# A selective scan feeding two attention layers: later groups' projection moved into the scan's steps, weight sums spread by a matmul, the last chunk's output steps moved closer

## The chip, the cores and the metric

The kernel runs on one core of one Trainium2 chip, in one launch. The metric is device time in microseconds, the median of several executions. One further execution was recorded by the hardware profiler; its time stands beside the median in the table below.

## The reference, cut to what matters

The input x has 32 sequences of 256 positions and 256 channels. A state-space block (a scan over positions) runs first, then two layers of windowed attention with a feed-forward part, and x is added at the end.

```
xr, gate = split(x @ W_in.T);  xr += t_emb
xc = silu(causal_conv4(xr) + b_conv)
xn = (xc - mean) / sqrt(var + eps) * ln_g + ln_b
Bm, Cm, dt = split(xn @ W_xproj.T);  dt = tanh(dt @ W_dt.T + b_dt) * 0.01
Ad = 1 + dt * -tanh(A_log);  Bd = Bm * min(|xn|, 1)
h_t = clip(h_{t-1} * Ad_t + Bd_t * xn_t, -10, 10);  y_t = C_t . h_t      # 256 steps
y = (y + D * xn) * silu(gate) @ W_out.T
for l in 0, 1:  y = ffn_l(attention_l(y))
return x + y
```

## The kernel before, in words

**Groups and chunks.** The 32 sequences are worked in 4 groups of 8 (GB). A group's scan has 256 steps, cut into 8 chunks of 32 (CH), and each chunk into two halves of 16 (hb). The partitions of the state h are 16 states by 8 sequences; its 512 columns are the inner channels. Group 0's scan has no attention beside it (`alone`); its tail and the scans of groups 1 to 3 run beside the attention of the group before.

**Slots.** `group_scan` writes an agenda: `at(s, what, ...)` puts a piece of work into slot s, where slot t is the slot of step t. Slots below 0 are preparation. Each group has two agendas; in each slot the pieces of the first come before those of the second. `scan_slots` merges the agendas of all groups, the next group 256 slots later, and `scan_to(s)` emits all slots up to s. This is the program order. The framework's planner then orders each engine's instructions by its own model of when operands and buffers are ready, in which it prefers program order; instructions wrapped in `keep_in_program_order` aren't overtaken. Loads that wait for nothing are drawn forward: weight loads (L978) written for slot 100 and later are issued from 18 us on. [...]

**Preparation of a chunk** (slots s0-43 to s0-4, s0 being the chunk's first step): `load_x` (L455, SP), `project` (L399, PE) into PSUM, `conv_in` (L469 to L483: DVE adds the conditioning, POOL the first tap), `conv_taps` (L489, DVE), `conv_th` (L499, ACT's Silu), `raw_sums` (L518, PE), then for each half j of the chunk's rows `norm_turn` (tp_x, L548, PE), `norm_stats` (L558 to L565, DVE and a power on POOL), `norm_shift` (L571), `norm_apply` (L579, ACT), `norm_affine` (L586 and L587, POOL), `norm_out` (L591 writes the rows to DRAM, xnd, through SP; L593 their squares on ACT). `length`, `figures`, `figures_out` (ps_st, L618), `figures_in` (L630 to L636), `decay_th` and `decays` (L643 to L661) make the steps' coefficients beta, ct and lim.

**Steps.** A step needs the normalised row of each sequence on the partitions of all 16 states. For 24 of 32 steps, `load_rows` (L685, xrep<-xnd, SP) fetches it by DMA six slots ahead; for the others `load_skip` (xq<-xnd, L745, SP) brings 16 rows at once and `spread_rows` (bx, L693, PE) spreads them. `scale_row` (L706, ACT) multiplies by beta, `step` (L716, one custom DVE instruction) makes h, and `read_out` (y, L728, PE) multiplies four steps' h by C.

**Output of a half or chunk:** `gated` (L779, DVE), `out_turn` (tz, L785, PE), `out_gate` (zT, L799, DVE), and after both halves `project_y` (ps_out, L808, PE), `copy_y` (L819, ACT) and `put_y` (L830, ys<-yo, ACT's queue). `load_res` (L956, res<-ys, SP) reads a sequence back for attention, whose first operation is `project_qkv` (ps_qkv, L989, PE).

**Weight sums.** Once, in preparation, `constants` folds W_dt into W_xproj (`fold_1`, `fold_2`: L266 to L284) and needs the column sums of the folded weights on the partitions of the states. `widen_w` (L290, POOL) copies 16 columns to 128 by repeating each 8 times; `sum_w` (tw, L301, PE) multiplies that by two columns (ones, and ln_b). This is done for three parts and two weight tables: six wide copies and 48 matmul instructions (an f32 matmul is two in the profile). `sums_w` (L310 to L312, DVE) reads the sums.

**Projection ahead.** While group 0's scan runs alone, the first half of `project` for the other three groups is done too: 48 units (u), each `ahead_project` (ps_a, L426: 8 matmul instructions), `ahead_copy` (L437, ACT) and `ahead_put` (ahead<-xs_a, L442, SP); every second unit first loads x (xa, L415, two DMAs on SP).

**From scan to attention.** `scan_to(S + DRAIN)` emits slots to 274, the eight `load_res` follow, then six rounds of `project` for attention with one slot each, and then attention stage by stage. Group 1's remaining slots are spread evenly over 114 stages.

Of the kernel before, what the change touches and what calls it, by code (L numbers as in the profile page):

```python
# [20 lines left out]
S = 256  # L21
# [3 lines left out]
NC_ = DI // P  # L25
NS = 16
GB = 8
# [3 lines left out]
NQ = 4  # L31
# [21 lines left out]
def bc(ap, axis, n):  # L53

    ap = ap.unsqueeze(axis)
    shape = list(ap.shape)
    shape[axis] = n
    return ap.broadcast_to(shape)
# [15 lines left out]
def kernel(  # L74
# [147 lines left out]
    def program(ctx, exact):  # L222
# [14 lines left out]
        def constants(at):  # L237
# [25 lines left out]
            def fold_1():  # L263
                td = bank(ps_w, "w", "td")
                for c in range(NC_):
                    nc.tensor.transpose(  # L266
                        td[0:NS, c * P : (c + 1) * P], tmp["wx"][:, c, 2 * NS :], ident
                    )
                wdT = work("swp", "wdT", 3)
                nc.vector.tensor_copy(wdT[0:NS], td[0:NS])  # L270
                tmp["wdT"] = wdT

            def fold_2():
                td = bank(ps_w, "w", "td2")[:, 0 : NC_ * NS].rearrange(
                    "p (c n) -> p c n", c=NC_
                )
                for c in range(NC_):
                    nc.tensor.matmul(
                        td[:, c], tmp["wdT"][0:NS, c * P : (c + 1) * P], tmp["dt"],
                        start=True, stop=True,  # L280
                    )
                wx = tmp["wx"]
                nc.vector.tensor_copy(wx[:, :, 2 * NS :], td)
                nc.vector.tensor_mul(wx_sb[:, :, 0 : 3 * NS], wx, bc(tmp["g"], 2, 3 * NS))  # L284

            def widen_w(i, k):
                t = ap_.tile([P, NC_, NS, GB], FP, tag="swp", name="wide", bufs=3)
                src = (wx_sb, tmp["wx"])[k]
                tc.keep_in_program_order(
                    nc.gpsimd.tensor_copy(t, bc(src[:, :, i * NS : (i + 1) * NS], 3, GB))  # L290
                )
                tmp["wide"] = t

            def sum_w(i, k):
                if (i, k) == (0, 0):
                    tmp["tw"] = bank(ps_w, "w", "tw")[:, 0:12].rearrange(
                        "p (i k n) -> p i k n", i=3, k=2
                    )
                t = tmp.pop("wide")
                for c in range(NC_):  # L300
                    nc.tensor.matmul(  # L301
                        tmp["tw"][:, i, k],
                        t[:, c].rearrange("p n b -> p (n b)"),
                        tmp["cols"][:, c, :],
                        start=(c == 0),
                        stop=(c == NC_ - 1),
                    )

            def sums_w():
                nc.vector.tensor_copy(wsum, tmp["tw"][:, :, 0, 0])  # L310
# [44 lines left out]
            at(-43, load_w)  # L355
            at(-34, fold_1)
            at(-32, fold_2)
            for n in range(6):
                at(-28 + 2 * n, widen_w, n // 2, n % 2)
                at(-27 + 2 * n, sum_w, n // 2, n % 2)  # L360
            at(-14, sums_w)
            at(-19, decay_rate)
            at(-16, load_later)
# [13 lines left out]
        def group_scan(g):  # L377
# [205 lines left out]

            def norm_affine(c, j):
                xn = ck[c]["xn", j]
                nc.gpsimd.tensor_mul(xn, xn, lng_sb)  # L586
                nc.gpsimd.tensor_add(xn, xn, lnb_sb)  # L587

            def norm_out(c, j):
                xn = ck[c].pop(("xn", j))  # L590
# [111 lines left out]
            def scale_row(c, t):  # L702
                if by_tensor(t):
                    ck[c]["rep", t] = xp.tile([P, DI], FP, tag="xrep", name="xrep")
                bx = ck[c]["rep", t]
                scaled = nc.scalar.activation(  # L706
                    bx, ck[c].pop(("bx", t), bx), AF.Copy, scale=ck[c]["beta"][:, t : t + 1]
                )
                if not alone:

                    tc.keep_in_program_order(scaled)

# [140 lines left out]
            for c in range(NCH):  # L853
                for t in range(CH):
                    at(c * CH + t, step, c, t)
            for c in range(NCH):
                s0 = c * CH
                for hb in range(CH // TB):
                    s = s0 + hb * TB
                    for i in range(NI):  # L860
                        at(s + 4 * i + 5, read_out, c, hb, i)
                    at(s + 21, gated, c, hb)
                    at(s + 25, out_gate, c, hb)
                    at(s + 11, skip, c, hb)
                for ch in range(NC_):
                    at(s0 - 38 + 2 * ch, conv_in, c, ch)
                    at(s0 - 37 + 2 * ch, conv_taps, c, ch)
                    at(s0 - 36 + 2 * ch, conv_th, c, ch)
                    if not alone:
                        at(s0 - 35 + 2 * ch, conv_out, c, ch)  # L870
                for ch, s in enumerate((13, 16, 17, 18)):
                    at(s0 + s + 2, gate_th, c, ch)
                    if not alone:
                        at(s0 + s + 4, gate_out, c, ch)
                at(s0 - 25, raw_copy, c)
                at(s0 - 24, raw_turn, c)
                for j in range(NJ):
                    s = s0 - 26 + 4 * j
                    at(s + 2, norm_stats, c, j)
                    at(s + 4, norm_shift, c, j)  # L880
                    at(s + 5, norm_apply, c, j)
                    at(s + 6, norm_affine, c, j)
                    at(s + 9, norm_out, c, j)
                at(s0 - 11, length, c)
                at(s0 - 9, figures, c)
                at(s0 - 7, figures_in, c)
                at(s0 - 6, decay_th, c)
                at(s0 - 5, decays, c)
                at(s0 - 4, put_c, c, 0)
                at(s0 + 4, put_c, c, 1)  # L890
                for d in range(KM):
                    at(s0 + 45 + 2 * d, copy_y, c, d)
                    at(s0 + 46 + 2 * d, put_y, c, d)
            agendas.append({})
            for c in range(NCH):
                s0 = c * CH
# [19 lines left out]
                for hb in range(CH // TB):  # L916
                    s = s0 + hb * TB
                    at(s - 9 if alone else s + 7, load_skip, c, hb)
                    at(s + 23, out_turn, c)
                for d in range(KM):  # L920
                    at(s0 + 43 + 2 * d, project_y, c, d)

            if alone:
                n = (NG - 1) * NCH * 2
                for u in range(n):
                    s = -30 + u * (NCH * CH) // n
                    at(s - 5, ahead_load, u)
                    at(s, ahead_project, u)
                    at(s + 2, ahead_copy, u)
                    at(s + 4, ahead_put, u)  # L930
# [561 lines left out]
                done[0] = next(scan, 1 << 30)  # L1492


        DRAIN = 18
        for i, (kind, k) in enumerate(WEIGHTS):
            scan_to(100 + 8 * i)
            load_weights(0, kind, k)
        scan_to(S + DRAIN)
        for b in range(GB):  # L1500
            load_res(0, b)
        for w in range(NW):
# [135 lines left out]
```

## Time and profile before

| what | us |
|---|---|
| median of 3 runs (3616.05 to 3620.17) | 3618.64 |
| the profiled execution | 3624.1 |
| its span, first to last instruction | 3622.3 |
| step 0 (first L716) starts | 56.93 |
| step 32, 64, 96, 128 | 106.77, 155.84, 204.90, 254.81 |
| step 160, 192, 224 | 303.99, 352.11, 400.44 |
| step 256, group 1's first | 447.77 |
| first ps_qkv | 480.27 |

PE is TensorE's matmuls, PEld its weight loads, DVE VectorE, ACT ScalarE, POOL GpSimd, SP SyncE; SPq and ACTq are DMA issues on those queues. L716 is line 716 of the kernel. Lines of the chain of waits give start, length and what; lines of the timeline give start, length, engine, line, operation, names, shapes, count and, in brackets, idle time before.

### The profile page before, as it was taken

To read this page: it belongs to the slowest core of one execution; us is meant where nothing else is said; L and a number is where in the kernel's file an instruction comes from. 1 tells how busy PE (TensorE), PEld (TensorE's weight loads), DVE (VectorE), ACT (ScalarE), POOL (GpSimd) and SP (SyncE) were. 2 spreads that over 40 slices of the span, in tenths; PEclk is the share of its full clock that TensorE was granted. 3 is DMA by queue.
4 is the path that set the end of the run, shared out by engine and by line. 5 is a ranking of instruction groups with operands and counts; after the bars stand their busy time and mean duration, and the time that the engine had idled before them with its cause. 6 is when DMAs were issued, how large, how long until landed. Compare 5 with 4: busy or idle time off the path is not lost.

```text
span 3622.3 us, 56212 instructions
## 1 busy us (share of the span) xinstructions
PE 3510.2 (97%) x19548; PEld 2282.4 (63%) x19548; DVE 2666.1 (74%) x5049; ACT 2151.6 (59%) x3659; POOL 1801.9 (50%) x1746
## 2 busy tenths in 40 slices
PE   8999989999999999999999999999999999999999
PEld 5445335666666666666666666666666677777677
DVE  5888889888787877887787778877777545555553
ACT  3666656666666666666666666666666444544443
POOL 4333456545455555645455556455544454544551
PEclk8999989999999999999999999999999999999999
DMA  7888755445454645444454554544454112011111
GB/s 192 212 218 217 197 155 149 133 111 137 129 141 123 154 137 151 123 113 128 118 139 125 137 150 135 137 107 130 115 138 120 54 45 62 13 30 36 34 27 37
DMA packets 468763, 435.59 MB, mean 120 GB/s; under 512 B 228724, under 2 KB 308085, under 8 KB 468341
## 3 DMA queue, kind: packets, MB, share of 16 engines
q1 hardware_dynamic: 384018, 419.88, 42.9%
q10 hardware_dynamic: 84450, 12.01, 2.0%
q8 instruction: 158, 2.59, 0.3%
q14 instruction: 137, 1.11, 0.1%
HBM read 383.54 MB, written 46.66 MB: 119 GB/s over the span
## 4 chain that ended last, share of the span: by engine, by line
PE 63%; DVE 16%; DMA 7%; POOL 6%; ACT 4%; issue 3%; SPq 1%; ACTq 0%; DVEq 0%; POOLq 0%
PE ps_qkv L989 13%; PE pa L1351 13%; PE po_f L1378 7%; DVE h L716 6%; DMA xrep<-xnd 5%; PE ps_wo L1039 4%; PE y L728 4%; PE sc L1198 4%; PE ov L1247 3%; PE ps_out L808 3%; PE tr_qk L1028 2%; DVE acc L489 2%; ACT xrep L706 2%; PE rs L1228 2%; PE ps_in L399 2%
## 5 line engine op out<-in xcount | busy, mean ns | idle before, releaser
L716 DVE CUSTOM_DVE_ANT_0 h<-h,xrep,lim 128x512 f32<-128x512 f32 x1024 | 954.0, 932 | 233.7 <-ACT xrep L706 198.4
L706 ACT ACTIVATE xrep<-xrep,beta 128x512 f32<-128x512 f32 x960 | 674.0, 717 | 367.4 <-DMA xrep<-xnd 280.8
L989 PE MATMUL ps_qkv<-qkv,res 128*128 128x512 f32 x1536 | 718.6, 603 | 22.2 <-DVE ag L1369 9.9
L1351 PE MATMUL pa<-hT,w 128*128 128x256 f32 (+1 forms) x2816 | 680.1, 383 | 1.2 <-ACT oT L1254 0.4
L1351 PEld LDWEIGHTS pa<-hT,w 128*128 128x128 f32 (+1 forms) x2816 | 515.3, 188 | 147.1 <-issue 57.1
L1013 POOL TENSOR_TENSOR rot<-rot,swp 128x512 f32<-128x512 f32 x256 | 335.7, 1311 | 444.7 <-DVE swp L1010 339.0
L989 PEld LDWEIGHTS ps_qkv<-qkv,res 128*128 128x128 f32 x1536 | 281.7, 191 | 314.2 <-issue 241.8
L1021 POOL TENSOR_TENSOR rn<-ss,neg_half 128x8 f32<-128x8 f32 x256 | 459.5, 1795 | 17.9 <-DVE ss L1019 7.9
L728 PE MATMUL y<-h,ly 128*32 128x512 f32 x2048 | 346.5, 611 | 12.5 <-DVE h L716 11.4
L1303 POOL TENSOR_TENSOR rstd<-ve,neg_half 128x2 f32<-128x2 f32 x64 | 46.3, 723 | 608.2 <-DVE ve L1301 605.0
L1378 PE MATMUL po_f<-ag,w 128*128 128x256 f32 x1280 | 307.9, 388 | 4.9 <-DVE fo L1389 4.9
L1022 POOL TENSOR_TENSOR rot<-rot,rn 128x512 f32<-128x512 f32 x256 | 291.8, 1140 | 20.1
L1369 DVE SCALAR_TENSOR_TENSOR ag<-pa,b_sb,ag 128x256 f32<-128x256 f32 x320 | 152.6, 477 | 198.8 <-ACT ag L1362 198.6
L1378 PEld LDWEIGHTS po_f<-ag,w 128*128 128x128 f32 x1280 | 236.5, 191 | 69.2 <-issue 12.8
L1002 ACT ACTIVATE sq<-ps_qkv 128x512 f32<-128x512 f32 x256 | 151.7, 596 | 210.1 <-PE ps_qkv L989 148.9
L1362 ACT ACTIVATE ag<-pa,b_sb 128x256 f32<-128x256 f32 x320 | 150.1, 469 | 176.3 <-PE pa L1351 173.9
L489 DVE SCALAR_TENSOR_TENSOR acc<-xr,wc_sb,acc 128x256 f32<-128x256 f32 x384 | 193.4, 528 | 57.6 <-POOL acc L478 57.1
L1039 PE MATMUL ps_wo<-oT,wo 128*128 128x256 f32 x1024 | 231.7, 379 | 0.7 <-ACT ag L1362 0.7
L1005 DVE TENSOR_TENSOR rot<-ps_qkv,rc_sb 128x512 f32<-128x512 f32 x256 | 175.1, 684 | 77.0 <-ACT sq L1002 76.7
L1198 PE MATMUL sc<-qT,kT 64*128 64x128 f32 (+1 forms) x2048 | 220.5, 344 | 0.0
L1207 ACT ACTIVATE pT<-sc 128x512 f32<-128x512 f32 x384 | 208.5, 596 | 12.2 <-PE sc L1198 10.2
L1198 PEld LDWEIGHTS sc<-qT,kT 64*128 64x128 f32 x2048 | 150.8, 187 | 99.8 <-issue 92.7
(159 smaller groups left out, 5656.2 us busy)
## 6 DMA issues: line engine op xcount, KB each, us to landing
xrep<-xnd SPq DMA_DIRECT2D x960, 256.0 KB
rb<-inv SPq DMA_DIRECT2D x128, 256.0 KB
xnd<-xn SPq DMA_DIRECT2D x64, 256.0 KB
qkv<-in_wqkv_dram SPq DMA_DIRECT2D x24, 512.0 KB
ahead<-xs_a SPq DMA_DIRECT2D x48, 256.0 KB
xp<-ahead SPq DMA_DIRECT2D x48, 256.0 KB
xd<-xnd SPq DMA_DIRECT2D x192, 64.0 KB
w<-in_w_dram SPq DMA_DIRECT2D x80, 128.0 KB
```

What stands on the lines that cost most here:

```text
L489: nc.vector.scalar_tensor_tensor(acc, xr[:, :, k : k + CH], wc_sb[:, ch, k : k + 1], acc, ALU.mult, ALU.add,)
L706: scaled = nc.scalar.activation(bx, ck[c].pop(("bx", t), bx), AF.Copy, scale=ck[c]["beta"][:, t : t + 1])
L716: nc.vector._custom_dve(TENSOR_ADD_SAT, out=h_new, in0=state["h"], in1=bx, s0=ck[c]["lim"][:, 0, t : t + 1], s1=ck[c]["lim"][:, 1, t : t + 1],
L728: nc.tensor.matmul(ck[c]["y", hb][32 * q : 32 * q + 32, :], ly[hb % 2][:, 32 * t : 32 * t + 32], ck[c].pop(("h", hb * TB + t)), start=(i = ...
L989: nc.tensor.matmul(ps, res[b][:, k, t0 : t0 + W], wt["qkv", a][:, k], start=(k == 0), stop=(k == KM - 1),)
L1013: nc.gpsimd.tensor_add(rot, rot, swp)
L1021: nc.gpsimd.tensor_tensor(rn, ss, neg_half, ALU.pow)
L1022: nc.gpsimd.tensor_mul(rot, rot, bc(rn, 2, DH))
L1039: nc.tensor.matmul(po[:, d], wt["wo", 0][:, c, d * P : (d + 1) * P], oT[:, c, :], start=(c == 0), stop=(c == NC_ - 1),)
L1198: nc.tensor.matmul(banks[r][:, i, :], kT[rows, i0 + i, kw * W : (kw + 1) * W], qT[rows, i0 + i, kw * W :], start=self.apart, stop=self.apa ...
L1351: nc.tensor.matmul(dst[x], wt["w1", m][:, k, x], self.h[:, k], start=(k == 0), stop=(k == KM - 1),)
L1378: nc.tensor.matmul(self.po[:, d], wt["w2", 0][:, m, d * P : (d + 1) * P], self.ag[m], start=(m == 0), stop=(m == len(MCH) - 1),)
```

## The change

Five things, all in group 0's scan and its two ends.

1. *Weight sums.* `sum_w` now multiplies the 16 columns themselves by the two columns (48 matmul instructions with 16 columns of weights, into 16 partitions); `copy_w` copies the result to SBUF (DVE) and builds a 16x128 matrix of repeated unit columns (POOL); `spread_w` spreads the sums to 128 partitions with one matmul. Two PSUM copies in `fold_1` and `fold_2` go from DVE to ACT.
2. *Projection ahead.* Unit u stands in slot 2 + 246u/48 and no longer in slot -30 + 256u/48.
3. *Chunk 0 and 1.* The affine part for the second half of chunk 0's rows is on DVE; the first eight `scale_row` of chunk 0 are kept in program order; chunk 1's conv steps are two slots later.
4. *The last chunk's second half.* gated, turn and gate stand 19, 20 and 21 slots after its first step (21, 23 and 25 before); the projections 38 and 39 after the chunk's first step (43 and 45), copies 39 and 40 (45 and 47), puts 40 and 41 (46 and 48).
5. *To attention.* `load_res` follows slot 266, not 274. `DRAIN` for later groups is the same.

```diff
-                nc.vector.tensor_copy(wdT[0:NS], td[0:NS])
+                nc.scalar.copy(wdT[0:NS], td[0:NS])
...
-                nc.vector.tensor_copy(wx[:, :, 2 * NS :], td)
+                nc.scalar.copy(wx[:, :, 2 * NS :], td)
...
-            def widen_w(i, k):
...
-            def sum_w(i, k):
...
+            def sum_w():
+                tw = bank(ps_w, "w", "tw")[0:NS, 0:12]
+                for i in range(3):
+                    for k, src in enumerate((wx_sb, tmp["wx"])):
+                        for c in range(NC_):
+                            nc.tensor.matmul(
+                                tw[:, 4 * i + 2 * k : 4 * i + 2 * k + 2],
+                                src[:, c, i * NS : (i + 1) * NS],
+                                tmp["cols"][:, c, :],
+                                start=(c == 0),
+                                stop=(c == NC_ - 1),
+                            )
+                tmp["tw"] = tw
+
+            def copy_w():
+
+                t = ap_.tile([P, NC_, NS, GB], FP, tag="swp", name="wide", bufs=3)
+                tmp["of_state"] = t[0:NS, 0].rearrange("p n b -> p (n b)")
+                tmp["by_state"] = t[0:NS, 1].rearrange("p n b -> p (n b)")[:, 0:12]
+                nc.gpsimd.tensor_copy(t[0:NS, 0], bc(ident[0:NS, 0:NS], 2, GB))
+                nc.vector.tensor_copy(tmp["by_state"], tmp.pop("tw"))
+
+            def spread_w():
+                tw = bank(ps_w, "w", "tw")[:, 0:12]
+                nc.tensor.matmul(tw, tmp["of_state"], tmp["by_state"], start=True, stop=True)
+                tmp["tw"] = tw.rearrange("p (i k n) -> p i k n", i=3, k=2)
...
-            for n in range(6):
-                at(-28 + 2 * n, widen_w, n // 2, n % 2)
-                at(-27 + 2 * n, sum_w, n // 2, n % 2)
+            at(-20, sum_w)
+            at(-19, copy_w)
+            at(-18, spread_w)
...
-                nc.gpsimd.tensor_mul(xn, xn, lng_sb)
-                nc.gpsimd.tensor_add(xn, xn, lnb_sb)
+                e = nc.vector if alone and (c, j) == (0, 1) else nc.gpsimd
+                e.tensor_mul(xn, xn, lng_sb)
+                e.tensor_add(xn, xn, lnb_sb)
...
-                if not alone:
+                if not alone or (c == 0 and t < 2 * NQ):
 
                     tc.keep_in_program_order(scaled)
...
+            def soon(c, hb):
+
+                return alone and (c, hb) == (NCH - 1, CH // TB - 1)
+
...
-                    at(s + 21, gated, c, hb)
-                    at(s + 25, out_gate, c, hb)
+                    at(s + (19 if soon(c, hb) else 21), gated, c, hb)
+                    at(s + (21 if soon(c, hb) else 25), out_gate, c, hb)
...
-                    at(s0 - 38 + 2 * ch, conv_in, c, ch)
-                    at(s0 - 37 + 2 * ch, conv_taps, c, ch)
-                    at(s0 - 36 + 2 * ch, conv_th, c, ch)
+                    s = s0 - 36 if alone and c == 1 else s0 - 38
+                    at(s + 2 * ch, conv_in, c, ch)
+                    at(s + 1 + 2 * ch, conv_taps, c, ch)
+                    at(s + 2 + 2 * ch, conv_th, c, ch)
...
-                    at(s0 + 45 + 2 * d, copy_y, c, d)
-                    at(s0 + 46 + 2 * d, put_y, c, d)
+                    s, q = (s0 + 39, 1) if soon(c, 1) else (s0 + 45, 2)
+                    at(s + q * d, copy_y, c, d)
+                    at(s + 1 + q * d, put_y, c, d)
...
-                    at(s + 23, out_turn, c)
+                    at(s + (20 if soon(c, hb) else 23), out_turn, c)
                 for d in range(KM):
-                    at(s0 + 43 + 2 * d, project_y, c, d)
+                    s, q = (s0 + 38, 1) if soon(c, 1) else (s0 + 43, 2)
+                    at(s + q * d, project_y, c, d)
...
-                    s = -30 + u * (NCH * CH) // n
+                    s = 2 + u * (NCH * CH - 10) // n
                     at(s - 5, ahead_load, u)
...
-        DRAIN = 18
+        FIRST_DRAIN, DRAIN = 10, 18
...
-        scan_to(S + DRAIN)
+        scan_to(S + FIRST_DRAIN)
```

## The prediction

> **What bounds the kernel now.** I read four views in this order: the page's busy shares, sums by stretch of time, the chain of waits up to the scan's first step, and the timeline around the scan's end.
>
> ```profile
> PE 3510.2 (97%) x19548; PEld 2282.4 (63%) x19548; DVE 2666.1 (74%) x5049; ACT 2151.6 (59%) x3659; POOL 1801.9 (50%) x1746
> ...
> PEclk8999989999999999999999999999999999999999
> ```
>
> TensorE is nearly always busy and, after the first slices, at full clock. By stretches (columns: stretch, length, then busy time and count of PE, PEld, DVE, ACT, POOL, then clock, DMA share, GB/s):
>
> ```profile
> 0.00:56.93 56.93, 42.77 (x155) 33.51 (x156) 22.73 (x68) 12.35 (x23) 23.83 (x69) 0.78 0.68 182
> 155.84:204.90 49.06, 46.97 (x216) 24.85 (x216) 41.96 (x73) 32.06 (x59) 18.54 (x26) 0.97 0.85 215
> 400.44:447.77 47.33, 43.07 (x135) 13.80 (x134) 42.91 (x81) 28.08 (x48) 21.16 (x25) 1.00 0.65 176
> 560.00:1300.00 740.00, 714.46 (x4128) 462.91 (x4126) 613.40 (x1151) 477.62 (x824) 396.81 (x381) 0.99 0.50 133
> ```
>
> The first row is the warm-up before step 0 (56.93), then chunks 2 and 7 of the first scan (32 steps each, 47.3 to 49.9 us), then attention, where PE is busy 97%. So from the first ps_qkv (480.27) on, the end follows PE's work; before it, PE's work is cheap and waits set the time. What the change can win lies before 480. The chain of waits there (start, length, what):
>
> ```profile
> 32.75 1.50 PE tw L301 x8
> 34.25 0.95 PE tp_x L548 x4
> 35.20 1.50 PE tw L301 x8
> 36.70 3.62 PE ps_a L426 x8
> 40.32 3.20 PE tw L301 x16
> 43.53 3.64 PE ps_a L426 x8
> 47.19 0.59 ACT xs_a L437
> 47.80 0.32 SPq L442
> 48.77 3.89 DMA xq<-xnd
> ```
>
> The normalisation's second half (tp_x) sits behind weight sums and later groups' projection; then the first row load xq waits in SP's queue behind the put of a projected block (L442). In 28 to 48 PE has no gap, yet runs at half clock:
>
> ```profile
> 36.00:40.00 4.00, 4.00 (x12) 3.37 (x12) 0.85 (x3) 0.78 (x1) 2.54 (x4) 0.50 0.46 133
> ```
>
> **What the Trainium skill says.** (1) "TensorE: Matmul & The Clock Gate", Part 1: half rate is the default and a busy window of some 3.4 us lifts it. The trace agrees only in part: 20 us of full PE stayed at 0.50, with 2-column matmuls in between. (2) "SBUF — State Buffer", Who interferes with whom: a VectorE instruction with two SBUF inputs contends with a GpSimd one that reads SBUF. It agrees: three conv taps (L489) took 2.43 us at 21.96 beside the "wide" copies, where their usual 0.48 each makes 1.44. [...] Here landings take longer: xq 3.9, ys 4.0 to 6.1, xnd 4.0 to 4.6 us.
>
> **The change, part by part.**
>
> *Start.* (a) The wide copies and 48 sum matmuls (L301, some 1.5 us per 8 at half clock, 9.8 us) go. In come 48 matmuls with 16 columns of weights: L266's such loads take 90 ns, L728's eight matmuls 1.06 us, so 4.3 to 6.4 us, and for the spread under 1 us. They stand after the second tp_x and before ps_st, in PE time that falls idle; uncovered they would cost 4 to 6. (b) Five and a half units of ps_a (3.62 us each cold) leave the path, with their puts and most loads on SP. (c) Two PSUM copies move from DVE (0.67 and 0.22) to ACT, and the wide copies no longer hold up taps (1.0): the first half's tp_x, which ended at 27.63, ends 1.5 earlier, 26.1; ACT's copy may take some back.
>
> Then the chain in measured pieces. tp_x to apply took 3.26 (27.63 to 30.89): 29.4. The first affine on POOL 2.6: 32.1. The second half's statistics follow the first's shift on DVE (28.5 to 29.6); its power is queued on POOL behind that affine: 32.7 at the latest, 30.4 if it goes between the two. Shift 0.54, apply 0.78 (34.1), the affine now on DVE, two at about 0.68 (L779's price, the same size): 35.5. So xnd's second write is issued at 35.6 instead of 41.41. It lands 4.3 later, 39.9; xq follows at once, since no put of a projected block stands before it on SP: 40.0 instead of 48.77. xq took 3.9, spreading and scaling about 1.8 more: step 0 at 45.7, or 43.4 with the early power. I take 45, **12 us earlier**. Beta is not later: length to beta took 9.6 with 4 us of waiting for PE, so about 42. Ends: -6 (SP stalls on weight loads put before xnd; two L978 loads stood there) and -15. The new order constraint on the first eight scale_rows puts chunk 1's Silu behind them on ACT; raw_sums at slot 5 waits for that, later by at most one 0.42 us Silu per row. Conv of chunk 1 is two steps later and has idle DVE to use before step 0.
>
> *Body.* The 48 units now lie in slots 2 to 243 rather than -30 to 221. Between step 0 and 255 there are 5.5 more: 10.6 us of PE (1.92 warm), 3.1 of ACT, 2 MB of DMA, and on SP three loads and 5.5 puts (L442 waited 15.7 us over the 42 there are, so 2 us). Four of them fall into chunk 7, which had none: there PE's work without its gaps is 8.5 (y) + 4.0 + 3.9 + 2.8 + 2.4 + 2.1 + 1.3 + 0.7 = 26 us of 47, so 8 more fit; DVE (42.9 of 47.3) gets nothing. I take +2 for it and +2 for the other chunks, where PE is at 45 to 47 of 49. **+4**, ends 0 and +9.
>
> *Last chunk and drain.* After the last step the work is y, gated, turn, gate, project, copy, put; then load_res waits for the puts.
>
> ```profile
> 457.37 0.66 DVE L799 TENSOR_TENSOR zT<-tz,sg 128x512 f32<-128x512 f32 x1
> ```
> ```profile
> 465.15 0.37 ACTq L830 DMA_DIRECT2D ys<-yo  x1
> ```
> ```profile
> 475.19 0.59 SPq L956 DMA_DIRECT2D res<-ys  x1
> ```
>
> gated ran at 453.19 and needs y, complete near 451. With turn and gate one slot apart zT comes near 454, 3.4 earlier; the two projections come one slot after another and the second put 5.5 earlier, 459.6. It lands after 5.2: 464.8. load_res now follows slot 266, and SP is there in time (the row load for step 272 went out at 460.2). So res is requested at 465 instead of 475.2 and first ps_qkv comes **10 us earlier**. Price: row loads for steps 273 on queue behind load_res on SP for some 4 us; steps of group 1 stall, PE has nothing to lose there. Eight slots of group 1's scan move into attention: y 8.5 + ps_in 4.0 + ps_out 3.9 + raw, turns, figures 4.5 = 21 us of PE per 32 steps, so **+5.5** for 8. Net -4.5; ends -9 (PE's gaps near 500 swallow the slots) and +2.
>
> **Sum.** -12 + 4 - 10 + 5.5 = -12.5. The profiled execution took 3624.1 (span 3622.3 and 1.8 around it): 3611.6. It lies 5.5 above the median 3618.64 of the runs shown, so 3606.1 there.
>
> **The rivals.** *It is paid back in the body.* SP's order keeps the start at -6 and the PE-dense chunks pay nearly all 10.6 us of moved projection: -6 + 9 - 4.5 = -1.5, 3617. For: PE at 46.97 of 49.06; ACT waits 83.6 us for row loads in 57 to 390, so a fuller SP tells. Against: DVE, whose step chain sets the pace, gets no work.
> *Slower: half clock in the first chunk.* PE rests before step 0, so step 0 may find it at half clock. A chunk needs about 42 us of warm PE work in 49; at half clock 10 us of it lose about 7. From 27 us of half clock on it takes back the 12.5 and 7 more. For: the 20 us at 0.50 above. Against: later chunks dip to 0.93 on average and recover within some 7 us. At 30 us: +22, 3628.
> *It doesn't do what it says.* The projection depends on nothing in the scan, and weight loads written for slot 100 on are issued at 18 us; if the planner draws ps_a forward as well, only the sums' 4 us are won, with no cost in the body: -8.5, 3610. Against: ps_a stood in slot order on PE before.
>
> **Chances.** Forecast 0.65 (alone 3597 to 3614), paid back 0.17, half clock 0.10, drawn forward 0.08. The range 3595 to 3617 leaves out half clock and about half of the paid-back case. About 0.2% (7.2 us) is what a measurement of this kernel tells from no change. Below 3611.4: most of the forecast and of the last case, 0.66; within: 0.24; slower: 0.10.
>
> **What would show it.** Step 0 near 45 with the chain of waits free of tw and ps_a and xq following xnd at once; ps_a until some 430; chunks 0 to 6 within 1 us of before; ys put 5 us and res 10 us nearer to step 255; from ps_qkv to the end about 5 us longer than 3142. Wrong if xq still stands behind L442 or L978, if clock stays at 0.50 past 70, or if the chunks lengthen by over 1.5 us each.

## The result and the profile after

The changed kernel takes 3640.63 us (median of 5 runs, 3635.52 to 3642.26), the kernel before 3618.64: ratio 1.0059 [1.0046, 1.0072]. It is 0.6% slower, where 0.3% faster was forecast. The profiled execution took 3635.52 (span 3633.4), 11.4 above that of before. Line numbers from L399 on are 4 to 12 higher than before (L716 is now L721, L989 is L1001, L956 is L968).

The two traces differ by these pieces, each from the first instruction of the operation named:

| piece | before | after | difference | predicted |
|---|---|---|---|---|
| start to step 0 | 56.93 | 47.95 | -9.0 | -12 |
| step 0 to step 256 | 390.8 | 400.1 | +9.3 | +4 |
| step 256 to first ps_qkv | 32.5 | 24.9 | -7.6 | -10 |
| first ps_qkv to the 17th sequence's | 805.3 | 825.3 | +20.1 | +5.5, all that follows included |
| the rest of the span | 2336.7 | 2335.2 | -1.5 | |

The page of after has nearly the same busy shares; PE's is one point lower:

```profile
PE 3488.4 (96%) x19550; PEld 2267.2 (62%) x19550; DVE 2662.4 (73%) x5050; ACT 2149.1 (59%) x3661; POOL 1807.0 (50%) x1739
...
PEclk8999989999999999999999999999999999999999
```

By stretches of after (warm-up, chunk 2, chunk 7, attention; columns as in the prediction):

```profile
0.00:47.95 47.95, 23.88 (x121) 15.67 (x122) 24.00 (x70) 9.91 (x20) 18.32 (x62) 0.79 0.74 205
149.03:197.12 48.09, 43.10 (x196) 24.31 (x196) 40.86 (x75) 30.60 (x55) 20.59 (x26) 0.93 0.84 216
399.25:448.05 48.80, 42.32 (x162) 18.13 (x160) 43.80 (x81) 29.30 (x52) 21.83 (x27) 0.93 0.75 206
560.00:1300.00 740.00, 709.37 (x4076) 458.03 (x4075) 608.46 (x1142) 468.68 (x814) 400.85 (x383) 0.99 0.49 134
```

The warm-up is 9 us shorter and PE is busy 23.88 us in it, not 42.77: the projection has left and the weight sums are short. In attention PE is busy 709.37 of 740 us, where it was 714.46. The chain of waits up to step 0 of after:

```profile
24.91 1.39 PE tw L291 x48
...
26.62 0.57 PE tw L310 x2
...
28.24 0.42 PE tp_x L552
...
33.53 1.60 POOL xn L592
...
42.58 0.55 POOL acc L482
43.16 0.48 DVE acc L493
...
44.83 1.29 DVE acc L493 x3
46.15 1.56 DVE acc L493
47.73 0.42 ACT xc L503
```

ps_a is gone from the chain, as foreseen, and the 48 weight-sum matmuls take 1.39 us. New at its end are chunk 1's conv taps (acc, xc), which stand ahead of the first scaled rows. At the other end of the scan, the timeline of after:

```profile
454.41 0.68 DVE L804 TENSOR_TENSOR zT<-tz,sg 128x512 f32<-128x512 f32 x1
...
463.03 0.37 ACTq L835 DMA_DIRECT2D ys<-yo  x1
...
466.85 5.16 SPq L968 DMA_DIRECT2D res<-ys  x8
```

Step 256 starts within 0.3 us of before, so the lines compare directly: the last put goes out 2.1 us earlier (465.15 before), res 8.3 us earlier (475.19). But what follows is longer. The first two sequences (48 ps_qkv instructions) and the next 14, before and then after:

```profile
480.27:545.57 65.30, 57.54 (x255) 25.14 (x256) 53.90 (x100) 32.81 (x58) 42.02 (x40) 0.85 0.50 136
545.57:1285.57 740.00, 715.11 (x4131) 463.95 (x4129) 615.37 (x1152) 476.56 (x824) 403.48 (x388) 0.99 0.51 135
```
```profile
472.94:542.04 69.10, 51.89 (x244) 25.82 (x244) 48.45 (x86) 35.92 (x67) 41.80 (x35) 0.88 0.36 110
542.04:1298.34 756.30, 725.66 (x4163) 466.46 (x4161) 626.41 (x1175) 480.11 (x834) 411.88 (x393) 0.99 0.50 135
```

PE's busy time in both rows together rises from 772.7 to 777.6, by 4.9. The rest are gaps: time in which no matmul runs is 32.6 us before (7.8 in the first row, 24.9 in the second) and 47.8 after (17.2 and 30.6). So in the first two sequences PE is busy 5.6 us less and has 9.4 us more gaps; in the next 14 it is busy 10.6 us more and has 5.7 us more gaps. A part of the work moved from the first two to the next 14: 19 of the scan's steps start in the first two, where it was 22, and 254 in the next 14, where it was 245. The granted clock doesn't explain it: 0.85 and 0.99 in the two rows before, 0.88 and 0.99 after.

The 4.9 are near the 5.5 that the prediction gave for the eight carried slots. But PE's busy time is a rough measure of work: between start_closer and start_end below the same eight slots make 8.2 us, and between the same two with half of the row loads left out it falls by 2.3.

PE's longest waits in the first two sequences, before and then after:

```profile
PE tr_qk L1028 <- POOL rot L1022: 5.2, 3, 2.2
```
```profile
PE tr_qk L1040 <- POOL rot L1034: 10.5, 3, 5.2
PE ps_st L623 <- DVE rhs L614: 5.6, 1, 5.6
```

### The profile page after: what moved, and what is told of

The parts are those of the page before. It is cut to its first block, busy times and chain, and to the rows that moved or that the text cites. A ratio compares the mean times of both kernels' runs of the same rounds, so it can differ in the third digit from the quotient of the medians.

```text
span 3633.4 us, 56199 instructions
## 1 busy us (share of the span) xinstructions
PE 3488.4 (96%) x19550; PEld 2267.2 (62%) x19550; DVE 2662.4 (73%) x5050; ACT 2149.1 (59%) x3661; POOL 1807.0 (50%) x1739
## 4 chain that ended last, share of the span: by engine, by line
PE 57%; DVE 20%; POOL 7%; DMA 7%; ACT 5%; issue 4%; SPq 0%; ACTq 0%; DVEq 0%; POOLq 0%
PE ps_qkv L1001 12%; PE pa L1363 12%; DVE h L721 7%; PE po_f L1390 6%; DMA xrep<-xnd 5%; PE ps_wo L1051 4%; PE y L733 4%; PE sc L1210 3%; PE ov L1259 3%; DVE acc L493 3%; PE ps_out L813 2%; ACT xrep L711 2%; POOL rn L1033 2%; PE tr_qk L1040 2%; POOL acc L482 2%
## 5 line engine op out<-in xcount | busy, mean ns | idle before, releaser
L721 DVE CUSTOM_DVE_ANT_0 h<-h,xrep,lim 128x512 f32<-128x512 f32 x1024 | 948.4, 926 | 251.2 <-ACT xrep L711 216.9
L1001 PE MATMUL ps_qkv<-qkv,res 128*128 128x512 f32 x1536 | 716.8, 602 | 17.3 <-DVE ag L1381 9.8
L1001 PEld LDWEIGHTS ps_qkv<-qkv,res 128*128 128x128 f32 x1536 | 280.9, 191 | 308.8 <-issue 242.4
L1034 POOL TENSOR_TENSOR rot<-rot,rn 128x512 f32<-128x512 f32 x256 | 291.8, 1140 | 20.1
L1390 PEld LDWEIGHTS po_f<-ag,w 128*128 128x128 f32 x1280 | 236.5, 191 | 78.8 <-issue 13.6
L1219 ACT ACTIVATE pT<-sc 128x512 f32<-128x512 f32 x384 | 208.3, 596 | 13.2 <-PE sc L1210 11.3
L1051 PEld LDWEIGHTS ps_wo<-oT,wo 128*128 128x128 f32 x1024 | 195.5, 191 | 31.4 <-DVE ve L566 3.0
```

What stands on the lines that cost most here:

```text
L721: nc.vector._custom_dve(TENSOR_ADD_SAT, out=h_new, in0=state["h"], in1=bx, s0=ck[c]["lim"][:, 0, t : t + 1], s1=ck[c]["lim"][:, 1, t : t + 1],
L1001: nc.tensor.matmul(ps, res[b][:, k, t0 : t0 + W], wt["qkv", a][:, k], start=(k == 0), stop=(k == KM - 1),)
L1034: nc.gpsimd.tensor_mul(rot, rot, bc(rn, 2, DH))
L1051: nc.tensor.matmul(po[:, d], wt["wo", 0][:, c, d * P : (d + 1) * P], oT[:, c, :], start=(c == 0), stop=(c == NC_ - 1),)
L1390: nc.tensor.matmul(self.po[:, d], wt["w2", 0][:, m, d * P : (d + 1) * P], self.ag[m], start=(m == 0), stop=(m == len(MCH) - 1),)
```

## The experiments

Three parts were separated. The **start part** is the edits 1 and 3 of the diff (weight sums, chunk 0's affine, order of the first rows, chunk 1's conv). The **projection** is edit 2. The **end part** is edits 4 and 5: closer output steps and attention begun after slot 266. All runs, in us; "17th" is the stretch from the first ps_qkv to the 17th sequence's, "gaps" PE's time without a matmul in it, both of the profiled execution. The kernel before was measured again beside each of four groups of runs, and the ratio is to those measurements: their medians were 3617.95 (the first four runs under after), 3621.14 (ahead_wide, start_closer, end_burst, end_all_groups), 3617.63 (ahead_half, closer_14, closer_26, end_pool) and 3615.84 (only_closer and the two halfrows). So a few us between medians of different groups say nothing; compare such runs by their ratios:

| run | median | ratio to before | step 0 | step 256 | first ps_qkv | 17th | gaps |
|---|---|---|---|---|---|---|---|
| before | 3618.64 | | 56.93 | 447.77 | 480.3 | 805.3 | 32.6 |
| after | 3640.63 | 1.0059 [1.0046, 1.0072] | 47.95 | 448.05 | 472.9 | 825.3 | 47.8 |
| only_start | 3615.11 | 0.9993 [0.9983, 1.0003] | 46.11 | 440.88 | 473.6 | 806.0 | 33.7 |
| start_ahead | 3625.72 | 1.0020 [1.0013, 1.0027] | 46.73 | 449.77 | 482.7 | 801.3 | 35.2 |
| start_end | 3633.23 | 1.0036 [1.0026, 1.0046] | 46.76 | 441.70 | 467.5 | 827.9 | 50.1 |
| only_end | 3643.06 | 1.0061 [1.0041, 1.0081] | 52.27 | 451.17 | 477.1 | 830.0 | 49.2 |
| ahead_wide | 3618.54 | 0.9993 [0.9985, 1.0001] | 48.60 | 447.39 | 479.8 | 801.1 | 31.5 |
| ahead_half | 3620.38 | 1.0008 [0.9999, 1.0016] | 47.07 | 440.50 | 474.7 | 799.2 | 32.6 |
| only_closer | 3614.88 | 0.9993 [0.9983, 1.0003] | 52.71 | 446.06 | 473.4 | 802.8 | 31.5 |
| start_closer | 3612.11 | 0.9979 [0.9973, 0.9986] | 47.40 | 442.98 | 469.8 | 801.3 | 31.7 |
| closer_14 | 3626.30 | 1.0021 [1.0011, 1.0030] | 48.15 | 439.38 | 465.0 | 820.5 | 44.0 |
| closer_26 | 3617.11 | 0.9998 [0.9990, 1.0006] | 48.03 | 443.65 | 481.9 | 799.2 | 36.2 |
| end_burst | 3627.24 | 1.0023 [1.0012, 1.0034] | 48.27 | 434.65 | 460.0 | 821.7 | 42.7 |
| end_all_groups | 3643.19 | 1.0071 [1.0054, 1.0088] | 45.49 | 440.38 | 465.8 | 823.3 | 50.0 |
| end_pool | 3633.52 | 1.0043 [1.0027, 1.0059] | 47.56 | 440.47 | 465.7 | 826.5 | 46.5 |
| closer_halfrows | 3586.68 | 0.9913 [0.9894, 0.9931] | 47.62 | 441.69 | 468.4 | 801.1 | 29.9 |
| end_halfrows | 3593.36 | 0.9936 [0.9919, 0.9954] | 45.79 | 441.93 | 466.2 | 806.4 | 37.5 |

**Which part costs.** The edits undone for each run:

```diff
 # start_ahead: the end part undone (and only_start)
-        FIRST_DRAIN, DRAIN = 10, 18
+        FIRST_DRAIN, DRAIN = 18, 18
-                return alone and (c, hb) == (NCH - 1, CH // TB - 1)
+                return False
 # start_end: the projection undone (and only_start, only_end)
-                s = 2 + u * (NCH * CH - 10) // n
+                s = -30 + u * (NCH * CH) // n
 # only_end: the start part undone too
-                nc.scalar.copy(wdT[0:NS], td[0:NS])
+                nc.vector.tensor_copy(wdT[0:NS], td[0:NS])
...
-                    s = s0 - 36 if alone and c == 1 else s0 - 38
+                    s = s0 - 38
```

> The kernel before with the first part alone: weight sums spread by a matmul, the two copies on ACT, chunk 0's second affine on DVE, the order constraint, chunk 1's conv two slots later. All theories: step 0 earlier by 3 to 5 (projection still on the path), nothing lost later: 3613 to 3616. If it is slower than before, the order of the planner decides and not the work.

> The changed kernel with its end undone: the last chunk's output steps and the 274 slots ahead of attention as before. Theory 1 (the handover costs: attention begun eight slots earlier meets a first stage in which POOL is the bound, and idles there and later; net some +11 of the +22): about 3627 to 3630, first ps_qkv near 481, and PE's idle time between the first ps_qkv and the 17th sequence back from 47 to some 31. Theory 2 (the body's +9 is the cause and the end gains its 4.5): slower still, about 3645. Theory 3 (the planner's order shifts by chance with every edit): anywhere within 15 of both.

> The changed kernel with the later groups' projection back in its slots from -30 on. Theory 1 (handover): still slow, 3630 or more: the start loses some of its gain, the body gets its 9 back. Theory 2 (moved projection costs 9 in the body): about 3631 or below, with chunks of 48 to 49.5 and step 0 near 52 to 54.

> The kernel before with the end alone: last chunk's output steps closer and attention after slot 266. Theory 1: first ps_qkv some 7 to 10 earlier and the end 5 to 12 later than before (3624 to 3631), idle PE between the first ps_qkv and the 17th sequence up by 10 or more. Theory 2: 4 to 5 faster, 3614.

The end part alone costs what the whole change costs (3643.06; 12 us more than the upper end that was expected for it). Beside the start part it costs 18.1 (start_end less only_start). The projection costs 10.6 (start_ahead less only_start) or 7.4 (after less start_end; 8.3 by the ratios). The start part alone gains 2.8 by the medians, which can't be told from nothing: its interval reaches 1.0003.

**Closer steps or early attention.** start_closer keeps the closer steps and begins attention after slot 274 again; only_closer is that without the start part.

```diff
-        FIRST_DRAIN, DRAIN = 10, 18
+        FIRST_DRAIN, DRAIN = 18, 18
```

> The kernel before with the start and the last chunk's closer output steps, but attention after slot 274 as before. Theory A (the loss is attention's early beginning: eight more slots of group 1's scan to carry through 114 stages): no loss, 3612 to 3618, first sequences and the stretch from the first ps_qkv to the 17th sequence at 806 as in the run with the start alone. Theory B (the closer steps disturb the last chunk and what follows): 3625 or more.

> The kernel before with the closer output steps of the last half chunk alone, attention begun after slot 274 as before. If they gain what start_closer is ahead of only_start (3 us at the first ps_qkv, kept to the end): 3613 to 3617. If attention's start is set by slot 274 and not by the puts: 3618 as before.

The one number 10 or 18 makes 21 us, by the medians (3633.23 and 3612.11) and by the ratios. The closer steps are no harm: with them the first ps_qkv is 4 us earlier than in only_start, and the end of the span 5.6. only_closer's interval still reaches 1.0003; start_closer is faster than both kernels, and of the versions that leave nothing out the fastest. Nor is it chance of the planner's order, which every edit moves: with whole row loads and attention begun after slot 274 or 282, the stretch to the 17th sequence is 799.2 to 806.0 us in all eight versions, and after slot 266 821.7 to 830.0 in all six.

**Where the slots run.** Both runs are start_end with one edit more. end_burst puts the eight carried slots all into attention's first stage, so that from then on scan and attention stand to each other as before. end_all_groups keeps slots and stages shifted by eight for all groups (and `soon` true for all), with the old number of slots per stage.

```diff
 # end_burst
-                scan_to(s0 + (2 * S + DRAIN - s0) * (t + 1) // reload)
+                scan_to(s0 + 8 + (2 * S + DRAIN - s0 - 8) * (t + 1) // reload)
 # end_all_groups
-                return alone and (c, hb) == (NCH - 1, CH // TB - 1)
+                return (c, hb) == (NCH - 1, CH // TB - 1)
-        FIRST_DRAIN, DRAIN = 10, 18
+        FIRST_DRAIN, DRAIN = 10, 10
```

> Start and end without the moved projection, attention after slot 266, but the eight carried slots are all run within attention's first stage, so that from there on the scan keeps the pace and place it had before (2.19 slots a stage, not 2.26). Theory A1 (the carried slots are dear because the denser pace meets full engines in sequences 4 to 12): the loss there goes, ps_qkv of the 17th sequence comes 803 to 810 after the first, 3612 to 3618 in all. Theory A2 (an early attention phase is dear in itself, POOL being the bound of its first stages): still 820 or more after the first, 3630. Theory A3 (planner's chance): neither.

> Start and end without the moved projection, and every group's last chunk gets the closer output steps, with ten slots of drain for all groups: attention begins after slot 266 and the scan of group 1 has to be at 522 by stage 114, so the pace is the old 2.19. Theory A1: 3608 to 3614, no loss in sequences 4 to 12. Theory A2 and A3: 3630 or so, as with the end for group 0 alone.

In end_burst the middle comes back: its stretch after the first two sequences is 740.7, that of start_end 758.2, of only_start 740.6. Of the 17.5 us less than in start_end, 9.9 are PE's busy time and 7.6 gaps. But the whole stretch is 821.7, as "A2" expected, and not 803 to 810: the first two sequences take 81.0 us in place of 65.4, more than the 13.6 by which the first ps_qkv came earlier. (The profiled execution lies 6.7 below its median and has 6.2 of the 13.6 from before step 256; where the rest of the median's loss lies, this trace doesn't show.) So the middle gets its loss back when the eight slots are taken out of it. That takes their work out too, so this run alone doesn't part place from amount. end_all_groups shows that the number of slots per stage is not it: with the old number its stretch is 823.3, and it loses more in later groups (2349.9 us in the rest of the span; the other versions with whole rows take 2334.7 to 2338.5).

**How far.** closer_14 and closer_26 begin attention after slots 270 and 282.

```diff
-        FIRST_DRAIN, DRAIN = 18, 18
+        FIRST_DRAIN, DRAIN = 14, 18        # closer_26: 26, 18
```

> The start part and the closer output steps, with attention begun after slot 270: half way between start_closer (slot 274, 3612) and start_end (slot 266, 3633). Theory of a price per slot (each slot of group 1 carried into attention costs about 2.6 us more than its start gains, in a straight line): half the loss, 3622 to 3624. Theory of place (what costs is which slot's work meets which stage of attention): off that line, either within 3 us of 3612 or at 3630 and more, with the loss again in sequences 5 to 12. My price in the prediction (0.69 us of PE a slot, less what the earlier start gains) gives 3610.

> The same with attention begun after slot 282, eight slots later than start_closer. Price per slot in a straight line: 3612 - 21 = 3591, with the first ps_qkv some 10 us later than 470 and the stretch from there to the 17th sequence 30 us shorter than its 331. Place: 3612 or slower, since the later start costs about 10 and the eight slots give back only some 5.5: 3617.

No straight line: the stretch to the 17th sequence is 799.2, 801.3, 820.5 and 827.9 for slots 282, 274, 270 and 266. Most of the loss comes between 274 and 270. PE's busy time in it grows at each step (762.9, 769.6, 776.5, 777.8); the gaps jump (36.2, 31.7, 44.0, 50.1). closer_14's median, 3626.30, met neither expectation: it is above the straight line and below what "place" gave. Beginning earlier than slot 274 has stopped paying; later costs at the first ps_qkv what it came later by (12.1) and gives 2.1 back.

**POOL in the first stage.** The waits on POOL's rot suggested that POOL bounds it. end_pool moves the affine part of group 1's chunks 1 and 2 to DVE.

```diff
-                e = nc.vector if alone and (c, j) == (0, 1) else nc.gpsimd
+                e = nc.vector if alone and (c, j) == (0, 1) or g == 1 and c in (1, 2) else nc.gpsimd
```

> The start and end parts together (start_end, 3633.2), with the affine part of the normalisation of group 1's second and third chunk on DVE in place of POOL. If attention's first stage is bound by POOL, whose rotations of q and k share it with that affine part: PE's gaps in the first two sequences fall from 17 us to 10 or less, and the time to 3626. If POOL only shows in the chain of waits without setting the end, or the loss is in sequences 5 to 12 alone: 3631 to 3636, the gaps in the first two sequences unchanged.

The gaps of the first two sequences fall from 17.0 to 12.4, less than expected if POOL bounds them, and the median doesn't move (3633.52). POOL's share of the affine is a part of the first stage's gaps, not what sets the end. The run also gives DVE the affine's work, and the stretch behind the first two sequences grows by 1.4 us; so a gain there may have been lost here.

**Late rows.** In sequences 3 to 16 of after 26 of 30 us of PE's gaps end on DVE, and DVE's own waits name the scan's rows. Of start_closer and then of start_end, in sequences 7 to 14 (columns: engine, waiting and releasing instruction, us, times, longest):

```profile
DVE h L721 <- ACT xrep L711: 14.5, 13, 2.9
```
```profile
DVE h L721 <- ACT xrep L711: 20.3, 19, 2.8
```
```profile
ACT xrep L711 <- DMA xrep<-xnd: 41.0, 21, 5.6
```
```profile
ACT xrep L711 <- DMA xrep<-xnd: 47.2, 25, 4.4
```

The suspicion: while a step at the head of DVE's order waits for its row, attention's work behind it waits too. To tell cause from company, half of the row loads are left out in the scans of groups 1 to 3 in both variants; odd steps scale the row of the step before, so their state isn't the reference's.

```diff
-                if by_tensor(t):
+                odd = not alone and t % 2 == 1
+                if by_tensor(t) or odd:
...
-                    bx, ck[c].pop(("bx", t), bx), AF.Copy, scale=ck[c]["beta"][:, t : t + 1]
+                    bx, ck[c]["rep", t - 1] if odd else ck[c].pop(("bx", t), bx), AF.Copy, scale=ck[c]["beta"][:, t : t + 1]
...
-                    if not by_tensor(t):
+                    if not by_tensor(t) and (alone or t % 2 == 0):
                         at(s0 + t - 6, load_rows, c, t)
```

> The start and end parts (start_end, 3633), with half of the row loads left out in the scans of groups 1 to 3: an odd step scales the row of the step before it, so that its state is not the reference's; scaling and steps stay. If late rows make the gaps in sequences 5 to 12: the wait of the steps for their rows falls from 20.3 us in them to under 10, the gaps of sequences 3 to 16 fall from 33 us to 23 or less, and the difference to closer_halfrows is that of the first two sequences and the carried work alone, 10 to 12. If the rows' wait only goes along with another order: the difference stays at 18 to 24.

> The same leaving-out with attention begun after slot 274 (start_closer, 3612). Both theories: a little faster than start_closer, 3600 to 3612, since the steps' waits on rows fall here too; it is the partner of end_halfrows.

The difference between the two starts falls from 21.1 to 6.7 us, less than the 10 to 12 expected. Sequences 3 to 16 of start_closer and start_end, then of closer_halfrows and end_halfrows:

```profile
533.40:1271.10 737.70, 714.10 (x4131) 462.89 (x4129) 615.75 (x1155) 478.28 (x826) 405.48 (x390) 0.99 0.52 135
537.20:1295.40 758.20, 725.11 (x4162) 466.54 (x4160) 625.64 (x1175) 479.86 (x834) 411.96 (x393) 0.99 0.52 134
```
```profile
535.60:1269.50 733.90, 712.41 (x4130) 462.29 (x4128) 616.49 (x1157) 479.95 (x827) 405.99 (x390) 0.99 0.36 91
534.90:1272.60 737.70, 716.48 (x4162) 463.75 (x4160) 620.32 (x1172) 484.69 (x836) 409.90 (x394) 1.00 0.36 92
```

The gaps, length less PE's busy time, are 23.6 and 33.1 with whole rows and the same, 21.5 and 21.2, with half. So without half of the row traffic the shifted place opens no gaps in the middle; 4.1 us of busy time stay. (In the first two sequences it still does: 8.4 and 16.3.) The way there is not the one expected. ACT's wait for loads fell by two thirds in the shifted variant, but the steps' wait for scaled rows hardly did (end_halfrows, same sequences):

```profile
DVE h L722 <- ACT xrep L712: 18.8, 20, 3.4
```
```profile
ACT xrep L712 <- DMA xrep<-xnd: 16.6, 6, 7.6
```

I had expected under 10 for the first. And in closer_26, which has no loss in the stretch to the 17th sequence, the steps wait as long for rows in sequences 7 to 14 as in start_end:

```profile
DVE h L721 <- ACT xrep L711: 19.9, 16, 3.1
```

Row traffic is thus needed for the gaps in the middle, but how long the steps wait for rows doesn't account for them. What does is open: it can be other transfers that queue with the rows. Leaving loads out also changes when row buffers come free and so the planner's order, which this pair can't separate. closer_halfrows itself is 13 us faster than the 3600 expected of it at best.

**The projection.** ahead_wide is only_start with the units spread from slot -30 to 240, beginning as before and ending as after; ahead_half is start_ahead without half of each unit's matmuls (what is put ahead is then not the whole projection).

```diff
 # ahead_wide
-                s = -30 + u * (NCH * CH) // n
+                s = -30 + u * (NCH * CH + 20) // n
 # ahead_half
-                    for k in range(KM):
+                    for k in range(1):
...
```

> The start alone, and the projection's units begun at slot -30 as before but spread to slot 241 (5.75 slots apart, not 5.33): about 3 units leave chunks 0 to 6 for chunk 7. Theory P (each unit in a full chunk costs its 1.9 us of PE, and chunk 7 has room): step 256 some 4 us earlier than with the start alone, 3611. Theory Q (the units' cost is in the planner's order and SP's stalls, wherever they stand): no change or slower than 3615.

> The start part with the moved projection (start_ahead, 3625.7, steps 0 to 256 in 403.0 us), leaving out half of each projected block's products (four of eight matmul instructions a unit, so that what is put ahead for later groups is not the whole projection); loads, copies and puts stay. If PE's time is what the moved blocks cost in the body: steps 0 to 256 fall by 8 or more, to 395 or less. If it is the loads and puts on SP and the copies on ACT: 401 to 403.

Steps 0 to 256 take 394.8 in only_start, 403.0 in start_ahead and 393.4 in ahead_half, as expected if PE's time is what the units cost. But ahead_half takes matmuls out of all 48 units, not only out of the 5.5 that moved: at 1.92 us a unit an estimate of 46 us of PE's work, for 9.6 us of time. The granted clock differs too, 0.95 in the body of start_ahead and 0.99 in that of ahead_half. So it shows no more than that the units' products bear on the body's length; that the moved ones cost their 8.3 us by PE's time is not shown. PE has 31 matmuls more in the body of start_ahead than in that of only_start, but is busy 367.9 and 367.1 us. One wait that grew is that of the statistics for tp_x, which the planner had put behind ps_a, in only_start and then in start_ahead:

```profile
DVE st L562 <- PE tp_x L552: 5.8, 5, 1.2
```
```profile
DVE st L562 <- PE tp_x L552: 13.7, 7, 4.0
```

In ahead_half it stays (13.2), while ACT's wait for row loads falls from 106.9 to 82.0 in the body; which of these costs is open. ahead_wide's step 256 is 6.5 later than only_start's, 2.5 of it before step 0: spreading wider did not help.

## Why the prediction was wrong

The step that failed is the price of the carried slots, "**+5.5** for 8". It counted PE's work and put the gaps that the shift opens at nothing: it took for granted that the slots find room, "PE's gaps near 500 swallow the slots" even as its better end. (Its own sum, 21 us per 32 steps, gives 5.2 for 8.) PE's busy time did rise by 4.9. But the gaps rose by 15.2, 9.4 in the first two sequences and 5.7 in the next 14: +18.5 to the end of the span in place of 5.5. start_closer against start_end shows that the early beginning of attention is what costs. closer_14 shows that the loss is not one price for every slot, and end_halfrows that the gaps of the middle need the row loads; by what path is open.

Of some 24 us between the forecast and the measured change of the profiled execution (-12.5, +11.4), this step is 13.0; the body is 5.3, the start 3.0, the drain 2.4. Between the medians another 10.6 come in, because the profiled execution of before lay 5.5 above its median and that of after 5.1 below. The other steps:

- *Start*: the mechanism held up to the first row load: second write at 35.69 (35.6 predicted), xq next on SP at 37.90 (40.0), beta complete at 41.2 (42). Then the first row had to wait. "later by at most one 0.42 us Silu per row" had the danger in the wrong direction: chunk 1's conv stood ahead of the scaled rows and the step, on ACT and on DVE, and step 0 came at 47.95, not 45:

```profile
45.75 0.42 ACT L503 ACTIVATE xc<-acc 128x256 f32<-128x256 f32 x1 [5.75 <-DVE acc L493]
46.07 0.67 ACT L711 ACTIVATE xrep<-bx,beta 128x512 f32<-128x512 f32 x1
```

- *The base of the start*: 56.93 was the start of one execution. only_closer and only_end, with the start unedited and PE's order up to there the same, reached step 0 at 52.71 and 52.27. What differs is the granted clock; the second ps_a unit, at half clock in before and at full clock in only_closer:

```profile
36.56 3.76 PE L426 MATMUL ps_a<-xa,w_in_sb 128*128 128x256 f32 x8
```
```profile
34.93 1.97 PE L426 MATMUL ps_a<-xa,w_in_sb 128*128 128x256 f32 x8
```

  So some 4.5 of the 12 us were time that other executions don't lose. I carried the whole saving over to the median. That fits only_start, whose median gained 2.8 and not 11, though its steps 0 to 256 also take 394.8 and not 390.8.
- *Weight sums*: 1.39 us for 48 matmuls, against 4.3 to 6.4. They stand in PE's idle time, as foreseen, so the error had no effect.
- *Body*: +9.3, just beyond the upper end +9 that I gave. "ps_a until some 430" held (428.4); "chunks 0 to 6 within 1 us" did not: chunk 1 is 2.4 longer, chunk 5 1.5, chunk 6 5.1. In chunk 6 DVE waited 4.2 us once for a projected block's load (xp), the kind of wait that I had not priced. start_ahead shows that the projection move alone costs 8.3 there. At the start it gained nothing: step 0 is at 46.73 with it and 46.11 without, in one execution each. So once the weight sums were short, the units before step 0 seem to have lain in PE's idle time.
- *Drain*: -7.6 against -10. The output came 3 us earlier at zT as worked out, but the last put only 2.1 earlier, at 463.03, since project_y waited behind y and chunk 1's raw sums on PE; res was requested at 466.85 (465).
- *The steps behind the hand-over*: "row loads for steps 273 on queue behind load_res on SP for some 4 us" and "PE has nothing to lose there". The eight res took 5.16 us on SP. Steps 272 to 280, six slots behind the hand-over, took 35.7 us; before, the steps as far behind it, 280 to 288, took 31.9, and 23.2 in start_closer. So most of it is the pace of the steps once attention runs. But PE did lose there. Its three waits on rot in the first two sequences of after:

```profile
487.48 0.66 PE L1040 MATMUL tr_qk<-ident,rot 128*128 128x128 f32 x4 [1.81 <-POOL rot L1034]
494.27 1.12 PE L1040 MATMUL tr_qk<-ident,rot 128*128 128x128 f32 x4 [5.16 <-POOL rot L1034]
498.93 1.12 PE L1040 MATMUL tr_qk<-ident,rot 128*128 128x128 f32 x4 [3.54 <-POOL rot L1034]
```

  From 483 to 499 POOL is busy 15.6 of 16 us, with the rotations of q and k and 2.5 us of group 1's affine among them; PE is busy 5.5. A row that came late, step 275's, is not the reason: DVE waited 7.9 us for it from 496.8 to 504.7, while PE's waits on rot lay between 485.7 and 498.9. That the gaps of the first two sequences fall to 12.4 without the affine (end_pool) fits; what makes the rest was not tried by itself.
- *Rivals*: half clock in the first chunk did not decide: chunk 0 took 49.60 us (49.84 before). "Paid back in the body" had the body right (+9, measured +9.3), and that alone took back the start's 9.0; it had the start too small (-6), and kept the gain of the end. Neither had gaps in attention in it, where most was lost.

## What to carry to other kernels

Where the bounding engine is busy 97% in a later stage, moving work into that stage costs its engine time plus the gaps that the shift opens: price it by trying the shift alone. Here the interleaved work fitted one alignment better than those four and eight slots earlier, and nothing in the sums of work said so. Ask first whether an earlier start is worth its place: here one constant, 10 or 18, made 21 us, while the closer steps without it cost nothing. And before taking a saving from a profiled execution to the median, ask how much of what is saved is particular to that execution, such as a cold clock.

## What the runs showed of the hardware

- With the same order of matmuls on PE up to step 0, the granted clock was 0.50 in all of 28 to 48 us in one execution (before). In two others it was already 1.00 in 28 to 32 us (only_end) and 0.94 in 32 to 36 us (only_closer), and step 0 came 4 us earlier. "TensorE: Matmul & The Clock Gate", Part 1, of the Trainium skill lets a few microseconds of busy PE lift the clock; in the execution in which it did not rise, PE was busy without a gap from 28 to 48 us.
- A matmul with 16 columns of weights and 2 moving columns cost 29 ns (48 in 1.39 us in after), against some 190 ns for one with 128 columns of weights (8 in 1.50 us in before), both at a granted clock of 0.50.
- Leaving out half of the row loads of three scans, 256 KB each, made the kernel faster by about 0.66% (start_closer 0.9979 and closer_halfrows 0.9913 of before; some 24 us). In sequences 3 to 16 of after no wait of PE is put down to a row load. How much of this is the transfers themselves and how much the order that changed with them was not separated.
